# Layer 2's 3x3 convolution re-tiled: three groups of 128 rows, a pair of 58, four image rows at a time

## The chip, the cores and the metric

The kernel runs on one core of a Trainium2 chip. Its time is device time in microseconds for one execution, lower is better. Three executions of the kernel before took 20,867.39, 20,871.12 and 20,881.85 us; the median is 20,871.12 us.

## The reference

Four images of 48 channels and 256 x 256 pixels pass through four residual layers. Before each layer the image is normalised in groups of three channels (the statistics in the kernel). Layers 0, 1 and 3 are gated convolution blocks with 8 x 8 Fourier filters. Layer 2, the one that is changed, is this (cut):

```python
def _L2_conv_ref(x, w1_off, b1_off, w2_off, b2_off, w1_mod, b1_mod, w2_mod, b2_mod):
    integ = jnp.cumsum(jnp.cumsum(x, axis=-1), axis=-2)
    h1 = jax.nn.gelu(_conv(x, w1_off, b1_off, 1), approximate=False)   # 3x3, 48 -> 48
    sub = _conv(h1, w2_off, b2_off, 0)                                  # 1x1, 48 -> 4
    ...                                                                 # a box and its area per pixel
    m1 = jax.nn.gelu(_conv(x, w1_mod, b1_mod, 1), approximate=False)   # 3x3, 48 -> 48
    area = area * _conv(m1, w2_mod, b2_mod, 0)                          # 1x1, 48 -> 48
    A, Bt, Ct, D = four bilinear samples of integ at the box's corners
    return (A + D - Bt - Ct) / area
```

The two 3x3 convolutions share their input, so the kernel computes them as one with 96 outputs; the two 1x1 ones together have 52. All arithmetic is float32.

## The kernel before

Two streams of work are emitted into one program. Stream "a" runs layers 0 and 1 of images 0 to 3 and then layer 3 of all four. Stream "b" runs the first statistics, the weights of layer 1, and layer 2 of each image as soon as its layer 1 is done. `run` advances whichever stream has the smaller clock, a sum of the numbers that each stream yields. Each engine executes its own instructions in program order; the framework orders each engine's list, and some instructions are pinned to the order in which they were written (`pinned`). So layer 2 of an image lies beside layers 0 and 1 of the next one, and layer 2 of the last image beside layer 3. Stream a has five PSUM banks, stream b two (and one for weights).

Layer 2 first builds a table of integral sums in HBM (`sums`). Then it works in 32 pieces of eight image rows per image. For each piece:

- `look` loads, for four rows, the columns of the convolution: which of the 48 channels x 9 taps lie on which partition. `columns` (L290) puts taps of the first two image rows and 16 channels of the third on 112 partitions (tile A, used three times with its columns shifted by dx) and the other 32 channels of the third row with ten rows of masks on 106 partitions (tile B). It issues seven DMAs on ACT's queue (L301 to L305); the tiles have two buffers.
- `convolve` (L941) takes two image rows, 512 pixels: four matmuls of 512 columns (L947) with 112, 112, 112 and 106 rows into one bank, then a Gelu on ACT (L954).
- `project` (L961) multiplies the result with the 1x1 weights (L966) and adds the bias on DVE (L971).
- `boxes` turns the 52 numbers of each pixel into indices and weights; `gather` fetches sums from the table by indirect DMA on GpSimd's queue (L1037), 16 for each of four steps of a piece; `add` weights and adds them on DVE (L1048 to L1051); `finish` transposes the result (L1062) and adds it to the image (L1069).

In the steady loop, step h of piece n gathers for n, adds for the step before, and convolves rows 2h and 2h+1 of piece n+2; it projects the rows of the step before, and the last two rows of a piece at the start of the next piece, just before `boxes`. Odd steps load columns for piece n+3.

Layers 0 and 3 have a convolution of the same kind with another layout: `columns2` (L345) puts 32 channels of the third row on A, 128 partitions, and on B the other 16 channels, twice: 58 partitions for even rows and 58 for odd ones, at partitions 0 and 64. `convolve2` (L420) runs full matmuls (L427) and the tails of 58 rows (L435), two of which stand on different halves of the array. Its loads go to SP's queue (the line of `dma`, L227).

The weights are scaled by the statistics at each layer's start: `normalised_weights` for layer 2, `normalised_weights2` for layers 0 and 3. Both multiply a table of zeros and ones with the statistics (L285, L399) and another table into the mask rows (L335, L413). Layer 2's two tables are loaded once at the start of the program; those of layers 0 and 3 are loaded in each call (L394, L395), into memory that the weights' own preparation (`fused_weights`, ending at L386) used before.

Of the kernel before, what the change touches and what calls it, by code (L numbers as in the profile page):

```python
# [20 lines left out]
CP = 2 * C  # L21
PW = 258
# [36 lines left out]
def constants():  # L59
# [42 lines left out]
    sel = np.zeros((CP, 4, 112))  # L102
    tapsel = np.zeros((112, 4, 106))
    for g in range(4):
        for p in range(112 if g < 3 else 96):
            if g < 3:
                tap, ch = 3 * (p // 48) + g, p % 48
            else:
                tap, ch = 6 + p // 32, 16 + p % 32
            tapsel[p, g, 96 + tap] = 1  # L110
            sel[ch, g, p] = 1


    sel2 = np.zeros((CP, 4, 122))
# [8 lines left out]
    for p in range(48):  # L123
        sel2[32 + p % 16, 3, [10 + p, 74 + p]] = 1
        for q in (0, 64):
            tapsel2[10 + p, 3, q + 6 + p // 16] = 1
    sel2 = np.concatenate([sel2_full.reshape(CP, -1), sel2[:, 3]], 1)
# [35 lines left out]
    for a in range(2):  # L163
# [11 lines left out]
        "c_sel": sel,  # L175
        "c_tapsel": tapsel,
# [12 lines left out]
class Net:  # L189
    def __init__(self, ctx, tc, a, out):  # L190
        self.tc, self.nc, self.a, self.out = tc, tc.nc, a, out
        self.nimage = a["x"].shape[0] // C

        self.banks = {
            f: ctx.enter_context(tc.tile_pool(name="ps" + f, bufs=n, space=PSUM)) for f, n in (("a", 5), ("b", 2))
        }
        self.stream = "a"
        self.const = ctx.enter_context(tc.tile_pool(name="const", bufs=1))
        self.dram = ctx.enter_context(tc.tile_pool(name="dram", bufs=1, space=DRAM))
        self.stat = ctx.enter_context(tc.tile_pool(name="stat", bufs=2))  # L200
        self.n = 0
        nc, a = self.nc, self.a
        self.ident = self.load("c_ident", [128, 128])
        dft = self.load("c_dft", [128, 6, 128])
        self.f1, self.f2, self.a1, self.a2, self.rf, self.ri = (dft[:, i, :] for i in range(6))
        self.sel = self.load("c_sel", [CP, 4, 112])
        self.tapsel = self.load("c_tapsel", [112, 4, 106])
        self.group = self.load("c_group", [CP, CP])
        self.eps = self.const.tile([128, 1], F32, name="eps")
        nc.vector.memset(self.eps[:], 1e-5)  # L210
        self.zero = self.const.tile([CP, PW + 4], F32, name="zero")
        nc.vector.memset(self.zero[:], 0.0)
# [68 lines left out]
    def column_scales(self, mr, pool):  # L281

        ps = self.bank()
        for g in range(4):
            self.nc.tensor.matmul(ps[:112, 2 * g : 2 * g + 2], self.sel[:, g, :], mr[:], start=True, stop=True)  # L285
        t = pool.tile([112, 4, 2], F32, name=self.nm("ms"), tag="ms")
        self.nc.vector.tensor_copy(t[:].rearrange("p a b -> p (a b)"), ps[:112, 0:8])
        return t

    def columns(self, x, r0, n, pool):  # L290

        dma = self.nc.scalar.dma_start
        A = pool.tile([112, n, PW], F32, name=self.nm("A"), tag="A")
        B = pool.tile([106, n, PW], F32, name=self.nm("B"), tag="B")
        row = lambda dy, dx: slice(PW * (r0 + dy) + dx, PW * (r0 + dy + n) + dx)
        flat = lambda t, p0, p1: t[p0:p1].rearrange("p r c -> p (r c)")
        for dy in range(2):  # L300
            dma(flat(A, 48 * dy, 48 * dy + 48), x[0:48, row(dy, 0)])  # L301
        dma(flat(A, 96, 112), x[0:16, row(2, 0)])
        for dx in range(3):
            dma(flat(B, 32 * dx, 32 * dx + 32), x[16:48, row(2, dx)])
        dma(flat(B, 96, 106), self.a["c_inside"][:, PW * r0 : PW * (r0 + n)])  # L305
        return A, B

    def taps(self, AB, pick):

        A, B = AB  # L310
        return [pick(A, dx) for dx in range(3)] + [pick(B, 0)]

    def tap_rows(self):

        got = []
        for dx in range(3):
            got += [(0, 48, dx, dx, 0), (48, 48, dx, 3 + dx, 0), (96, 16, dx, 6 + dx, 0)]
            got.append((32 * dx, 32, 3, 6 + dx, 16))
        return got

    def normalised_weights(self, wb, n, mr, pool):


        nc = self.nc
        t = self.column_scales(mr, pool)
        W = pool.tile([112, 4, n], F32, name=self.nm("W"), tag="W")
        md = pool.tile([112, 4], F32, name=self.nm("md"), tag="md")
        nc.vector.scalar_tensor_tensor(md[:], t[:, :, 0], -1.0, t[:, :, 1], ALU.mult, ALU.mult)
        with self.pool("mt", 1) as sb:
            mt = sb.tile([112, 4, 106], F32, name=self.nm("mt"), tag="mt")  # L330
            ps = self.bank()
            for g in range(4):
                k = 112 if g < 3 else 96
                nc.vector.tensor_scalar(W[:k, g, :], wb[:k, g, :], t[:k, g, 1:2], None, ALU.mult)
                nc.vector.tensor_scalar(mt[:k, g, :], self.tapsel[:k, g, :], md[:k, g : g + 1], None, ALU.mult)  # L335
            for g in range(4):
                k = 112 if g < 3 else 96
                nc.tensor.matmul(ps[:106, :n], mt[:k, g, :], wb[:k, g, :], start=g == 0, stop=g == 3)
        nc.vector.tensor_copy(W[96:106, 3, :], ps[96:106, :n])
        return W  # L340

    def columns2(self, x, r0, n, pool):  # L345
# [4 lines left out]
        for dy in range(3):  # L350
            m = 48 if dy < 2 else 32
            self.dma(flat(A, 48 * dy, 48 * dy + m), x[0:m, row(dy, 0)])
        split = lambda v, q: v.rearrange("p (r q c) -> p r q c", q=2, c=PW)[:, :, q, :]
        for q in range(2):
            self.dma(B[64 * q : 64 * q + 10], split(self.a["c_inside"][:, PW * r0 : PW * (r0 + n)], q))
            for dx in range(3):
                p = 64 * q + 10 + 16 * dx
                self.dma(B[p : p + 16], split(x[32:48, row(2, dx)], q))
# [30 lines left out]
    def normalised_weights2(self, wb, n, mr, pool):  # L389
# [3 lines left out]
        with self.pool("nw", 1) as sb:  # L393
            sel = self.load("c_sel2", [CP, 506], sb)  # L394
            tapsel = self.load("c_tapsel2", [128, 4, 74], sb)  # L395
            ps = self.bank()
            for g in range(4):
                k = 128 if g < 3 else 122
                nc.tensor.matmul(  # L399
                    ps[:k, 2 * g : 2 * g + 2], sel[:, 128 * g : 128 * g + k], mr[:], start=True, stop=True  # L400
# [10 lines left out]
            for g in range(4):  # L411
                nc.vector.tensor_scalar(W[:, g, :], wb[:, g, :], t[:, g, 1:2], None, ALU.mult)
                nc.vector.tensor_scalar(mt[:, g, :], tapsel[:, g, :], md[:, g : g + 1], None, ALU.mult)  # L413
# [498 lines left out]
    def layer2(self, x, mr, y, table):  # L912
# [3 lines left out]
        with ExitStack() as ctx:  # L916
# [3 lines left out]
            wb = w.tile([112, 4, 96], F32, name="wb")  # L920
            for p0, m, g, t, c0 in self.tap_rows():
                self.dma(wb[p0 : p0 + m, g, :], a["L2_w1"][t, c0 : c0 + m, :])
            W = self.normalised_weights(wb, 96, mr, w)
# [10 lines left out]
            kk = [112, 112, 112, 106]  # L934
# [6 lines left out]
            def convolve(t, j):  # L941

                if j == 0:
                    t.sc = sb.tile([128, 16, 52], F32, name="sc", tag="sc", bufs=1)
                ps = self.bank()
                for g, of in enumerate(self.taps(t.G[j // 2], lambda G, d: G[:, 2 * (j % 2) : 2 * (j % 2) + 2, d : d + 256])):
                    m = nc.tensor.matmul(  # L947
                        ps[:96, :].rearrange("p (r c) -> p r c", c=256), W[: kk[g], g, :],
                        of[: kk[g]], start=g == 0, stop=g == 3,
                    )  # L950
                    if g == 0:
                        self.pinned(m)
                t.hm[j] = sb.tile([96, 512], F32, name="hm", tag="hm")
                nc.scalar.activation(t.hm[j][:], ps[:96, :], AF.Gelu, bias=b1[:])  # L954

            def look(t, h):

                if t is not None:
                    t.G[h] = self.columns(x, 128 * t.i + 8 * t.s + 4 * h, 4, cols)

            def project(t, j):  # L961

                ps = self.bank()
                for b in range(4):
# [4 lines left out]
                    if b == 0:  # L969
                        self.pinned(m)  # L970
                self.pinned(nc.vector.tensor_add(  # L971
                    t.sc[:, 4 * j : 4 * j + 4, :], ps[:, 0:208].rearrange("p (k e) -> p k e", e=52),
                    b2[:].unsqueeze(1).to_broadcast([128, 4, 52]),
# [110 lines left out]
            for j in range(4):  # L1084
                convolve(pieces[0], j)
                project(pieces[0], j)
                if j % 2:
                    look(pieces[1], j // 2)
            boxes(pieces[0])
            yield 30  # L1090
            for j in range(4):
                convolve(pieces[1], j)
                if j < 3:
                    project(pieces[1], j)
                if j % 2:
                    look(pieces[2], j // 2)
            yield 30
            last, done = None, None
            for n in range(len(pieces) + 1):
                t = piece(n)  # L1100
                for h in range(4):
# [12 lines left out]
                    if h == 0 and ahead is not None:  # L1114
                        project(ahead, 3)
# [6 lines left out]
                    if t is not None:  # L1122
                        last = (t, h, V)
                        if after is not None:
                            convolve(after, h)
                            if h % 2:
                                look(piece(n + 3), h // 2)
                            if h > 0:
                                project(after, h - 1)
# [242 lines left out]
```

## Time and profile before

| | us |
|---|---|
| median of three executions | 20,871.12 |
| the profiled execution | 20,882.08 |
| its span, first to last instruction | 20,880.3 |
| GpSimd's 8192 indirect DMAs (L1037), busy | 8,227.0 |
| layer 0's and 3's full matmuls (L427), busy | 5,547.3 |
| layer 0's and 3's 58-row tails (L435), busy | 1,271.5 |
| layer 2's convolution: three groups (L947, 112 rows), busy | 1,544.9 |
| layer 2's convolution: fourth group (L947, 106 rows), busy | 527.2 |
| layer 2's projections (L966), busy | 537.0 |
| layer 2's Gelus (L954), busy | 349.4 |

"Busy" is the time in which at least one instruction of the group ran. Matmuls are pipelined and overlap in the records, so a group's busy time is not the time it takes away from others; the step from one instruction's start to the next one's is nearer to that. PE is TensorE's matmuls, PEld its weight loads, DVE VectorE, ACT ScalarE, POOL GpSimd, SP the queue of SyncE; ACTq and SPq are the issuing of DMAs on these engines' queues. "[3.22 <-DVE xt L1069]" behind a line says that the engine stood idle for 3.22 us before it, until line 1069 on DVE had ended. The last layer 2 ends at about 19,840 us; then layer 3 of the last image runs alone.

| DMA queue | packets | MB | share of 16 engines |
|---|---|---|---|
| q1, issued by SP | 1,908,216 | 2084.50 | 38.2% |
| q0, issued by GpSimd | 452,560 | 1110.45 | 21.1% |
| q10, issued by ACT (the columns of layer 2) | 82,944 | 230.48 | 4.4% |

### The profile page before, as it was taken

How to read it: one execution, taken by the hardware profiler on the slowest of the kernel's cores; microseconds unless marked ns; L12 is line 12 of the kernel's file. 1: busy time of each engine (PE TensorE's matmuls, PEld its weight loads, DVE VectorE, ACT ScalarE, POOL GpSimd, SP SyncE). 2: the span in 40 equal slices, each digit the busy share in tenths (PEclk: the TensorE clock that was granted, in tenths of full speed). 3: DMA queues.
4: the chain of work that ended last, by engine and by line, in shares of the span. 5: the costliest groups of instructions: out<-in, count | busy, mean ns of one | idle time of the engine just before them, and what ended most of it. 6: DMA issues, size and time to landing. Idle time of an engine off the chain costs nothing.

```text
span 20880.3 us, 231985 instructions
## 1 busy us (share of the span) xinstructions
PE 18892.3 (90%) x79032; PEld 12001.4 (57%) x79032; DVE 10763.0 (52%) x21931; ACT 5909.3 (28%) x12275; POOL 8637.2 (41%) x8887
## 2 busy tenths in 40 slices
PE   7998798999878989998788899997888999999999
PEld 4565435666533346665433466654334787878888
DVE  4544322477765534677645447776554255555521
ACT  2333312344321123443311234433112211111111
POOL 1000000277754511777555216775552066666600
PEclk9899799999968999999689899996899999999999
DMA  4623886555588975555889755558897566666633
GB/s 114 135 55 82 233 217 194 137 132 134 132 235 230 241 207 139 130 134 127 233 230 240 219 133 130 133 127 229 236 239 225 137 150 151 158 152 160 151 76 74
DMA packets 2444896, 3440.27 MB, mean 165 GB/s; under 512 B 580102, under 2 KB 1997038, under 8 KB 2333179
## 3 DMA queue, kind: packets, MB, share of 16 engines
q1 hardware_dynamic: 1908216, 2084.50, 38.2%
q0 software_dynamic: 452560, 1110.45, 21.1%
q10 hardware_dynamic: 82944, 230.48, 4.4%
q8 instruction: 635, 10.40, 0.2%
q14 instruction: 541, 4.43, 0.1%
HBM read 2486.99 MB, written 802.77 MB: 158 GB/s over the span
## 4 chain that ended last, share of the span: by engine, by line
PE 65%; DMA 15%; DVE 7%; POOL 7%; issue 4%; SPq 1%; ACT 1%; DVEq 0%; ACTq 0%; POOLq 0%
PE ps L427 19%; POOL V L1037 7%; PE ps L947 6%; PE ps L728 5%; PE ps L435 4%; PE ps L741 4%; DMA ct<-cD 4%; PE ps L742 3%; PE ps L697 3%; PE ps L828 3%; DMA hD<-hs 2%; PE ps L1188 2%; DVE V L1050 2%; PE ps L815 1%; PE ps L966 1%
## 5 line engine op out<-in xcount | busy, mean ns | idle before, releaser
L1037 POOL DMA_INDIRECT V<-t,idx x8192 | 8227.0, 1004 | 4897.9 <-issue 2346.8
L427 PE MATMUL ps<-W,A 128*128 128x288 f32 (+1 forms) x24576 | 5547.3, 374 | 85.9 <-DMA A<-x 23.4
L427 PEld LDWEIGHTS ps<-W,A 128*128 128x128 f32 x24576 | 4281.6, 191 | 1226.6 <-issue 523.4
L227 POOL DMA_DIRECT2D X<-x x192 | 144.5, 757 | 4302.6 <-DMA x<-xt 3040.1
L1050 DVE TENSOR_TENSOR V<-V 128x1536 f32<-128x1536 f32 (+3 forms) x2048 | 1839.3, 900 | 19.2
L1048 DVE TENSOR_TENSOR V<-V,w 128x3072 f32<-128x3072 f32 x512 | 1713.3, 3346 | 35.9 <-DMA V<-t,idx 27.0
L728 PE MATMUL ps<-hg,ct 128*128 128x512 f32 x2304 | 1264.4, 676 | 417.5 <-DMA ct<-cD 339.5
L947 PE MATMUL ps<-A,W 112*96 112x512 f32 x3072 | 1544.9, 642 | 26.2 <-DVE xt L1069 21.5
L697 PE MATMUL ps<-win,xp 48*128 48x288 f32 x4096 | 1054.8, 594 | 547.9 <-DVE xp L684 232.4
L508 ACT COPY qkv<-ps 128x288 f32<-128x288 f32 x2048 | 769.9, 400 | 2641.1 <-PE ps L427 1258.4
L435 PE MATMUL ps<-W,B 58*128 58x288 f32 (+1 forms) x8192 | 1271.5, 391 | 26.1 <-DMA B<-x 13.8
L742 PE MATMUL ps<-yh,ht 65*128 65x512 f32 x2304 | 1163.1, 649 | 145.7 <-DMA yh<-ys 111.6
L531 DVE BATCH_NORM_STATS2 bs<-ps 128x6 f32<-128x96 f32 x2048 | 397.4, 251 | 1634.3 <-PE ps L529 1632.3
L741 PE MATMUL ps<-ys,tt 128*128 128x512 f32 x2304 | 1174.1, 632 | 27.6 <-DVE ys L732 25.7
L697 PEld LDWEIGHTS ps<-win,xp 48*128 48x128 f32 x4096 | 647.3, 259 | 924.3 <-ACT hs L704 291.9
L1168 DVE TENSOR_TENSOR gp<-gl,ps 128x192 f32<-128x192 f32 x1024 | 353.8, 351 | 1588.1 <-ACT gl L1167 1579.9
L728 PEld LDWEIGHTS ps<-hg,ct 128*128 128x128 f32 x2304 | 468.0, 211 | 1051.6 <-issue 949.1
L1167 ACT ACTIVATE gl<-ps 128x192 f32<-128x192 f32 x1024 | 332.7, 330 | 2529.4 <-PE ps L427 2245.4
L435 PEld LDWEIGHTS ps<-W,B 58*128 58x128 f32 x8192 | 762.4, 186 | 454.1 <-issue 346.4
L746 DVE TENSOR_TENSOR gt<-gl,ps 128x512 f32<-128x512 f32 x576 | 395.1, 687 | 1142.2 <-PE ps L742 1136.6
L947 PEld LDWEIGHTS ps<-A,W 112*96 112x96 f32 x3072 | 513.9, 176 | 731.4 <-issue 690.3
L742 PEld LDWEIGHTS ps<-yh,ht 65*128 65x128 f32 x2304 | 451.3, 199 | 794.3 <-issue 699.4
(186 smaller groups left out, 24654.4 us busy)
## 6 DMA issues: line engine op xcount, KB each, us to landing
hD<-hs SPq DMA_DIRECT2D x64, 4608.0 KB
hg<-hD SPq DMA_DIRECT2D x288, 1024.0 KB
gD<-gt SPq DMA_DIRECT2D x144, 1024.0 KB
gs<-gD SPq DMA_DIRECT2D x64, 2304.0 KB
V<-t,idx POOLq DMA_INDIRECT x8192
A<-x SPq DMA_DIRECT2D x512, 193.5 KB
xt<-x SPq DMA_DIRECT2D x256, 387.0 KB
A<-x ACTq DMA_DIRECT2D x512, 193.5 KB
```

The lines of the kernel that those rows point to most:

```text
L427: nc.tensor.matmul(to(q, b), A[:, r + q, 128 * b + g : 128 * b + g + 128], W[:, g, :], start=b == 0 and g == 0, stop=b == 1 and g == 2,)
L435: nc.tensor.matmul(to(q, b), B[p, r // 2, 128 * b : 128 * b + 128], W[p, 3, :], start=b == 1, stop=b == 0)
L508: nc.scalar.copy(t.qkv[:, 2 * q + b, :], banks[2 * b + q][:, 0:288])
L697: nc.tensor.matmul(ps[:, :288], xp[64 * h : 64 * h + 48, b, :], win[64 * h : 64 * h + 48], start=True, stop=True,)
L728: nc.tensor.matmul(ps[:].rearrange("p (s n) -> p s n", n=32), ct[:, c, :], hg[:, :, c, :], start=True, stop=True)
L741: nc.tensor.matmul(order(ps[:]), to[:, q, :], pick(yo, 128, q), start=True, stop=False)
L742: nc.tensor.matmul(order(ps[:]), ho[:, q, :], pick(yho, NZ, q), start=False, stop=True)
L828: nc.tensor.matmul(pp[:CP, :], pr[:, q, :], got[q][:], start=q == 0, stop=q == 2)
L947: m = nc.tensor.matmul(ps[:96, :].rearrange("p (r c) -> p r c", c=256), W[: kk[g], g, :], of[: kk[g]], start=g == 0, stop=g == 3,)
L1037: nc.gpsimd.indirect_dma_start(out=V[:, k, 4 * cr : 4 * cr + 4, :].rearrange("p e c -> p (e c)"), out_offset=None, in_=table, in_offset=ba ...
L1048: self.pinned(nc.vector.tensor_mul(Vm, Vm, wm.unsqueeze(2).to_broadcast([128, 64, 48])))
L1050: nc.vector.tensor_add(V[:, :, 0:n, :], V[:, :, 0:n, :], V[:, :, n : 2 * n, :])
```

## The change

Layer 2 now uses `columns2` and `normalised_weights2`, and the older functions go. `columns2` takes the queue on which it issues (ACT's for layer 2): three loads of A and, for each of two halves of B, a mask and three loads, 11 in all. `convolve` takes four image rows: into a first bank rows 0 and 2, into a second rows 1 and 3, each with three full matmuls of 128 rows and one tail of 58; the two tails stand together between the two sets of full ones. Two Gelus follow. `project` still takes one bank's 512 pixels and writes its sums in the order of the rows. In the loop, even steps convolve and load, odd steps project twice; a piece is projected entirely before the step in which `boxes` runs. The two tables are loaded once at the start, for all layers. Layer 2's weights take 15 loads instead of 12 and a memset.

```diff
@@ Net.__init__
-        self.sel = self.load("c_sel", [CP, 4, 112])
-        self.tapsel = self.load("c_tapsel", [112, 4, 106])
+        self.sel = self.load("c_sel2", [CP, 506])
+        self.tapsel = self.load("c_tapsel2", [128, 4, 74])
...
-    def columns2(self, x, r0, n, pool):
+    def columns2(self, x, r0, n, pool, dma=None):
+        dma = dma or self.dma
         A = pool.tile([128, n, PW], F32, name=self.nm("A"), tag="A")
         B = pool.tile([122, n // 2, PW], F32, name=self.nm("B"), tag="B")
...
@@ normalised_weights2
-            sel = self.load("c_sel2", [CP, 506], sb)
-            tapsel = self.load("c_tapsel2", [128, 4, 74], sb)
...
@@ layer2
-            wb = w.tile([112, 4, 96], F32, name="wb")
-            for p0, m, g, t, c0 in self.tap_rows():
+            wb = w.tile([128, 4, 96], F32, name="wb")
+            nc.vector.memset(wb[:, 3, :], 0.0)
+            for p0, m, g, t, c0 in self.tap_rows2():
                 self.dma(wb[p0 : p0 + m, g, :], a["L2_w1"][t, c0 : c0 + m, :])
-            W = self.normalised_weights(wb, 96, mr, w)
+            W = self.normalised_weights2(wb, 96, mr, w)
...
-            def convolve(t, j):
+            def convolve(t, h):
 
-                if j == 0:
+                if h == 0:
                     t.sc = sb.tile([128, 16, 52], F32, name="sc", tag="sc", bufs=1)
-                ps = self.bank()
-                for g, of in enumerate(self.taps(t.G[j // 2], lambda G, d: G[:, 2 * (j % 2) : 2 * (j % 2) + 2, d : d + 256])):
-                    m = nc.tensor.matmul(
-                        ps[:96, :].rearrange("p (r c) -> p r c", c=256), W[: kk[g], g, :],
-                        of[: kk[g]], start=g == 0, stop=g == 3,
-                    )
-                    if g == 0:
-                        self.pinned(m)
-                t.hm[j] = sb.tile([96, 512], F32, name="hm", tag="hm")
-                nc.scalar.activation(t.hm[j][:], ps[:96, :], AF.Gelu, bias=b1[:])
+                A, B = t.G[h]
+                ps = [self.bank() for _ in range(2)]
+                to = [p[:96, :].rearrange("p (r c) -> p r c", c=256) for p in ps]
+                for q in range(2):
+                    for g in range(3):
+                        m = nc.tensor.matmul(
+                            to[q], W[:, g, :], A[:, q:4:2, g : g + 256],
+                            start=q == 0 and g == 0, stop=q == 1 and g == 2,
+                        )
+                        if q == 0 and g == 0:
+                            self.pinned(m)
+                    if q == 0:
+                        for i in range(2):
+                            p = slice(64 * i, 64 * i + 58)
+                            nc.tensor.matmul(to[i], W[p, 3, :], B[p, :, 0:256], start=i == 1, stop=i == 0)
+                for q in range(2):
+                    t.hm[2 * h + q] = sb.tile([96, 512], F32, name="hm", tag="hm")
+                    nc.scalar.activation(t.hm[2 * h + q][:], ps[q][:96, :], AF.Gelu, bias=b1[:])
...
-                    t.G[h] = self.columns(x, 128 * t.i + 8 * t.s + 4 * h, 4, cols)
+                    t.G[h] = self.columns2(x, 128 * t.i + 8 * t.s + 4 * h, 4, cols, nc.scalar.dma_start)
...
@@ the loop of layer2
                     if h == 0 and ahead is not None:
-                        project(ahead, 3)
                         boxes(ahead)
...
                         if after is not None:
-                            convolve(after, h)
-                            if h % 2:
+                            if h % 2 == 0:
+                                convolve(after, h // 2)
                                 look(piece(n + 3), h // 2)
-                            if h > 0:
-                                project(after, h - 1)
+                            else:
+                                for j in range(2):
+                                    project(after, h - 1 + j)
                     yield 11
```

## The prediction

> **What bounds the kernel now.** I read the page's busy shares and its chain of waits first, then busy times by stretch, then TensorE's instructions one by one.
>
> ```profile
> PE 18892.3 (90%) x79032; PEld 12001.4 (57%) x79032; DVE 10763.0 (52%) x21931; ACT 5909.3 (28%) x12275; POOL 8637.2 (41%) x8887
> PE 65%; DMA 15%; DVE 7%; POOL 7%; issue 4%; SPq 1%; ACT 1%; DVEq 0%; ACTq 0%; POOLq 0%
> ```
>
> TensorE is busy 90% and carries 65% of the chain; the convolution to be changed (L947) is 5.8% of it. Layer 2 always runs beside something else, and what limits differs by stretch (span, PE, PEld, DVE, ACT, POOL, clock, DMA share, GB/s):
>
> ```profile
> 4000.00:5700.00 1700.00, 1625.56 (x6414) 1012.19 (x6414) 1184.44 (x2653) 673.78 (x1410) 1170.48 (x1149) 0.98 0.52 130
> 5700.00:6330.00 630.00, 464.48 (x1477) 247.96 (x1474) 397.15 (x683) 180.46 (x293) 344.36 (x357) 0.66 0.81 231
> 6330.00:7430.00 1100.00, 962.78 (x2229) 409.99 (x2227) 573.50 (x836) 184.68 (x304) 581.56 (x614) 0.90 0.91 237
> 16560.00:19700.00 3140.00, 3032.23 (x18721) 2498.80 (x18720) 1683.69 (x3016) 586.20 (x1319) 1983.37 (x2027) 0.98 0.66 154
> ```
>
> Beside layer 0 (first row) and layer 3 (last row) PE is busy 96%; beside layer 1's two parts (rows two and three) it is 74% and 88%, and DMA is nearly full. Rows one to three recur for two more images. The same view for L947's instructions alone counts 608, 168, 248 and 1024 of them in the four stretches (282, 108, 116 and 471 us of PE).
>
> Every float32 matmul is two records (two passes). L947 has 4096, and 16 make four image rows: 256 tiles of four rows, of which 3×38=114 lie beside layer 0, 3×10.5=31.5 and 3×15.5=46.5 beside layer 1, 64 beside layer 3.
>
> **The convolution.** Durations overlap, so the price is the step from one weight load to the next. The first two rows are L947 at full clock, the next two a pair of 58-row matmuls of layer 0, the last two one such matmul alone:
>
> ```profile
> 4526.58 0.16 PEld L947 LDWEIGHTS ps<-A,W 112*96 112x96 f32 x1 [0.27 <-issue]
> ...
> 4528.72 0.16 PEld L947 LDWEIGHTS ps<-B,W 106*96 106x96 f32 x1 [0.27 <-issue]
> ...
> 4026.61 0.30 PEld L435 LDWEIGHTS ps<-W,B 58*128 58x128 f32 x4 [0.79 <-issue]
> 4027.30 1.02 PEld L427 LDWEIGHTS ps<-W,A 128*128 128x128 f32 x5 [0.39 <-issue]
> ...
> 4470.03 0.29 PEld L435 LDWEIGHTS ps<-W,B 58*128 58x128 f32 x2 [0.39 <-issue]
> 4470.70 0.78 PEld L427 LDWEIGHTS ps<-W,A 128*128 128x128 f32 x4 [0.39 <-issue]
> ```
>
> 4526.58 to 4528.72 is five steps: 0.428 us for 512 columns. Layer 0's full matmuls of 288 columns step 0.243 us. The pair's four passes take 4027.30−4026.61=0.69 us: two steps of 0.243 plus 0.20, so the halves of the array run together; the lone one's two passes take 0.67, the same. The 0.20 is the price of going to half-array matmuls and back.
>
> Four rows cost 16×0.428=6.85 us now, and 12×0.428+(2×0.428+0.20)=6.20 after: 0.66 less. The compiled order of the changed kernel has 239 pairs side by side and 17 apart; those cost 2×1.06 instead of 4×0.428, 0.40 more. 239×0.66−17×0.40=151 us of PE, 0.59 per tile.
>
> A rule speaks against this: the Trainium skill, TensorEngine Tiling (Array Packing), Key Properties, says a change of tiling mode drains TensorE, with no figure; its Theoretical Speedup gives up to 2×. At 2× the sum would be 256×0.86=219 us; the rows with their 0.20 give 166 before the split pairs. I take the rows, because they contain the drain.
>
> What of it shortens the span:
> - Beside layer 0: 114×0.59=67 us. GpSimd is close behind (1170 us busy and 322 between gathers, of 1700; the chain in this stretch is 27% gathers), so I count 65%: 44.
> - Beside layer 3: 64×0.59=38; PE lines carry over 85% of its chain: 34.
> - Layer 1's first part: 31.5×0.59 at clock 0.66 instead of 0.98 is 28; PE idles 26% behind copies and stores, so half: 14.
> - Its second part: 46.5×0.59=27; loads of ct and yh hold PE, so 0.3: 8.
>
> Together 100.
>
> **Tables once.** Sixteen loads leave SP's queue. They matter where layer 3 begins:
>
> ```profile
> 17520.90 0.31 SPq L227 DMA_DIRECT2D c_sel_sb<-c_sel  x1
> 17521.26 0.42 SPq L227 DMA_DIRECT2D c_tapsel_sb<-c_tapsel  x1
> ...
> 17525.21 1.82 PE L399 MATMUL ps<-mr,c_sel_sb 96*128 96x2 f32 x8 [23.16 <-DMA c_tapsel_sb<-c_tapsel]
> ```
>
> The loads issue when L386 has ended (17,520.87), since they reuse its memory. L399 then waits 4.3 us for them and runs 1.8; both go. The other 17 us of the 23 is the weights' own loads and stays. PE waits so at three layer starts (54.2 us in all): 3×6=18. At the other starts no such wait shows: nothing; if one becomes the last wait, under 5 us each.
>
> **Loads of columns, on ACT's queue.** A look becomes 11 issues instead of 7:
>
> ```profile
> 4513.90 0.31 ACTq L301 DMA_DIRECT2D A<-x  x1
> 4514.25 0.43 ACTq L302 DMA_DIRECT2D A<-x  x1
> 4514.78 1.32 ACTq L304 DMA_DIRECT2D B<-x  x3
> 4516.14 0.37 ACTq L305 DMA_DIRECT2D B<-c_inside  x1
> ```
>
> Now 2×0.31+0.43+1.32+0.37=2.74 us; after, with six B at 0.44, two masks at 0.37 and three A, 4.4: +1.7 us × 256. Against it, Gelus come in twos and compiled table loads fall from 336 to 246: 90×1.28=115 us of ACT saved. Behind an issue stand layer 0's qkv and qs copies or layer 3's gl, and PE needs the banks they free. Four of the 11 stand ahead of the second Gelu, while PE still convolves; behind it 7 to 9 remain, where 6 are now: 0.4 to 1.3 us later. ACT is busy 40% of the first stretch, and PE waits there only 2.4 us for its largest item, qs. Ends: nothing, or 1.7×178=300 us if every issue beside layers 0 and 3 reaches PE. The waits are near nothing, so I take 25.
>
> Bytes fall: 218 rows of 4128 B become 128 of these and 232 of 1032, 900 to 768 KB. The Trainium skill, DMA: Bandwidth & Descriptors, Bandwidth, calls transfers under 64 KB descriptor-dominated and gives 0.68 us for 4 KB, 0.95 for 64 KB. An estimate from it: eight small ones of about 0.8 us replace three of about 1.1 and a mask, +2 us a look, and 46.5 looks fall where DMA is full: +100. The queue table says otherwise: ACT's queue moves 230.48 MB in 4.4% of the engines' time, SP's, with packets of 1.1 KB instead of 2.8, 2084.50 MB in 38.2%: 52 and 55 MB per percent. By that a look saves 132 KB, 0.56 us at 237 GB/s: 26 us there, half of it counted 10 with what PE saves already taken. I take the row; ends −26 and +100.
>
> **The rest.** A convolution takes both PSUM banks of its stream, then two projections follow one another. PE stands still for L1069's additions 21.5+31.2 us in all; where two transposes come just before two projections, the convolution no longer lies between them and 3.4 us of cover go, at 64 strips: from −20 (projections precede boxes by half a step) to +100; near the present waits, +15. GpSimd issues 12 more weight loads of 0.5 us, once per image three: +5. The projection's addition writes in another order with the same 208 values: nothing.
>
> **Sum:** −100−18−10+25+15+5=−83. The profiled execution took 20,882.1 us (span 20,880.3), 11 above the median of 20,871: 20,799 becomes **20,790**.
>
> **Rivals.**
> - *Gathers pace layer 0's stretches* (15%): nothing there, and the waits cost 60 instead of 45: −56−18−10+60=−24, 20,850. For it, GpSimd's 27% of the chain; against, PE's 96%.
> - *All of it counts* (15%): 67+38+28+20+18+10=181, waits near 10: 20,700.
> - *ACT's issues stop PE* (9%, slower): in each of 178 looks the copy behind the last issue is late, stream a's five banks run out, and PE stands for the 1.7 us: −128+303+20=+195, 21,065. It decides from 0.7 us per look. Against: ACT's slack.
> - *The pairs run in turn* (4%, the change not doing what it says): 0.20 more for 256 tiles, +51, and −28+45: 20,940. Against: the 0.69.
>
> My forecast has 57%. Faster: 0.57+0.15=0.72; within 0.2%, about what a measurement can tell: 0.15; slower: 0.13. The range 20,690 to 20,900 takes in the first two rivals and the smaller waits and leaves out the two slow ones.
>
> **What would show it.** The tails' four passes taking 1.06 us; PE about 150 us less busy; no wait of L399's successor on a table; PE's waits on qs, qkv and gl still small. A sum of such waits above 130 us, or a stretch beside layer 0 still 1700 long with PE less busy, would prove me wrong.

## The result, and the profile after

The changed kernel took 20,767.55 us (median of five runs, 20,746.18 to 20,843.95), the kernel before, run beside it, 20,871.12 (20,852.44 to 20,887.15): a ratio of 0.9953, 95% interval 0.9941 to 0.9965, or 104 us less. The forecast was 20,790. Its sum is nearly right and most of its terms are not, as the experiments show.

The page of the changed kernel, the lines that answer to the first two shown of before:

```profile
PE 18830.0 (91%) x79032; PEld 11956.8 (58%) x79032; DVE 10830.0 (52%) x21947; ACT 5784.0 (28%) x12185; POOL 8656.1 (42%) x8899
PE 72%; DMA 14%; DVE 6%; POOL 4%; issue 2%; SPq 1%; ACT 1%; ACTq 0%; DVEq 0%; POOLq 0%
```

TensorE is busy 62 us less, not 150. The stretches are compared from event to event, not at fixed times. First the kernel before, for its second image: layer 1's first, second and third part, then layer 0 of the third image, then all of layer 3 (columns as before: span, then PE, PEld, DVE, ACT, POOL, clock, DMA share, GB/s):

```profile
5699.30:6268.70 569.40, 410.46 (x1361) 225.35 (x1361) 365.21 (x626) 170.21 (x276) 317.19 (x328) 0.63 0.81 232
6268.70:7440.70 1172.00, 1017.58 (x2345) 433.27 (x2346) 609.65 (x898) 194.94 (x321) 609.43 (x643) 0.90 0.91 236
7440.70:7791.50 350.80, 299.25 (x1393) 186.73 (x1394) 126.01 (x270) 111.86 (x219) 14.12 (x20) 0.92 0.71 209
7791.50:9901.40 2109.90, 2026.43 (x8267) 1292.86 (x8266) 1344.03 (x3068) 825.54 (x1793) 1202.74 (x1189) 0.98 0.52 131
16198.00:20872.00 4674.00, 4491.49 (x28190) 3790.02 (x28190) 2051.34 (x3782) 893.73 (x2056) 2106.52 (x2159) 0.98 0.58 134
```

Then the changed one, the same five stretches:

```profile
5689.10:6240.70 551.60, 408.72 (x1360) 238.40 (x1360) 375.48 (x626) 173.19 (x277) 335.88 (x345) 0.62 0.86 243
6240.70:7418.80 1178.10, 1017.86 (x2336) 430.23 (x2336) 608.40 (x898) 193.90 (x320) 606.89 (x634) 0.89 0.91 232
7418.80:7747.50 328.70, 292.61 (x1386) 182.37 (x1387) 124.74 (x266) 111.47 (x218) 12.68 (x18) 0.95 0.72 216
7747.50:9848.00 2100.50, 2010.95 (x8280) 1276.76 (x8278) 1355.27 (x3076) 784.17 (x1764) 1189.18 (x1186) 0.98 0.52 129
16089.00:20758.00 4669.00, 4492.11 (x28229) 3783.80 (x28227) 2063.74 (x3791) 892.26 (x2060) 2112.51 (x2164) 0.97 0.59 133
```

Over all images the stretches changed so: layer 1's first part -47 us, its second +25, its third -68, layer 0 -20, layer 3 -6; with 2 us at the start these are the 115 between the two traces' ends. The third part, where no layer 2 runs, gave most. It ends with the next layer's weights, and there the loads of the tables stood. Layer 3, where the forecast put 52 us, gave almost nothing.

### The profile page after: what moved, and what is told of

It is laid out like the page before. It is cut to its first block, busy times and chain, and to the rows that moved or that the text cites. A ratio compares the mean times of both kernels' runs of the same rounds, so it can differ in the third digit from the quotient of the medians.

```text
span 20765.8 us, 232624 instructions
## 1 busy us (share of the span) xinstructions
PE 18830.0 (91%) x79032; PEld 11956.8 (58%) x79032; DVE 10830.0 (52%) x21947; ACT 5784.0 (28%) x12185; POOL 8656.1 (42%) x8899
## 4 chain that ended last, share of the span: by engine, by line
PE 72%; DMA 14%; DVE 6%; POOL 4%; issue 2%; SPq 1%; ACT 1%; ACTq 0%; DVEq 0%; POOLq 0%
PE ps L353 22%; PE ps L361 5%; PE ps L876 5%; PE ps L654 4%; POOL V L974 3%; PE ps L668 3%; PE ps L667 3%; DMA ct<-cD 3%; PE ps L623 3%; PE ps L754 3%; PE ps L1120 2%; PE ps L901 2%; PE ps L811 2%; PE ps L505 2%; DMA A<-x 2%
## 5 line engine op out<-in xcount | busy, mean ns | idle before, releaser
L876 PE MATMUL ps<-A,W 128*96 128x512 f32 x3072 | 1483.5, 619 | 3.0 <-issue 3.0
L876 PEld LDWEIGHTS ps<-A,W 128*96 128x96 f32 x3072 | 487.2, 168 | 853.4 <-issue 839.6
L658 DVE COPY ys<-ps 128x512 f32<-128x512 f32 x576 | 397.2, 690 | 1086.0 <-PE ps L654 897.3
```

Source lines behind the costliest of these rows:

```text
L876: m = nc.tensor.matmul(to[q], W[:, g, :], A[:, q:4:2, g : g + 256], start=q == 0 and g == 0, stop=q == 1 and g == 2,)
```

## The experiments

All ran beside the kernel before on the same chip. Four chips were met: one for experiments 1 to 4 and one for 5 to 8, both with a granted clock of about 0.92 (before: 20,884.8 and 20,857.2 us), and one each for 9 and 10 and for 11 and 12, which granted 0.84 (25,694 and 25,632 us). On these last two more than the clock differs: TensorE's waits sum to about 5,200 us, against 1,900 in the changed kernel's first trace, and for 2,100 of them the profile names nothing that was waited for. So what a whole kernel shows there need not hold on the other chips. Across chips ratios are compared; where differences of medians are given too, this is said.

**1. Tables once, on the kernel before.**

```diff
@@ Net.__init__
-        self.tapsel = self.load("c_tapsel", [112, 4, 106])
+        self.tapsel = self.load("c_tapsel", [112, 4, 10])
+        self.sel2 = self.load("c_sel2", [CP, 506])
+        self.tapsel2 = self.load("c_tapsel2", [128, 4, 74])
...
@@ normalised_weights2
-            sel = self.load("c_sel2", [CP, 506], sb)
-            tapsel = self.load("c_tapsel2", [128, 4, 74], sb)
+            sel, tapsel = self.sel2, self.tapsel2
```

> The kernel before, layer 2 unchanged, with the two tables for paired columns loaded once (the old tapsel kept as its ten non-zero columns, so that all four tables fit). The prediction's theory: only the waits at three layer-3 starts go, -18 us, about 20,853. Its rival, from the two traces: the loads also held up VectorE where layer 0 follows layer 1 (L386's product stands on VectorE's queue ahead of stream b's sums), and the four stretches after layer 1 lost 68 us and the turns between layer 3's images 16: -70 to -85 us, 20,785 to 20,800. A third: the 68 us belong to the new loop or the layout, and this gives -13 to -20.

20,634.8 us, ratio 0.9890 (0.9874 to 0.9906): 250 us faster than the kernel before beside it, beyond every expectation. By stretch, the third parts and the starts in them gave -62 us, and layer 1's second part, which the edit does not touch, went from 902.3, 1172.0, 1179.2 and 1162.7 to 841.6, 1127.8, 1126.4 and 1122.9. The first of the four has no layer 2 beside it. This called for an explanation of its own (5 to 9).

**2. The changed kernel with those two loads back in each call of layers 0 and 3.**

```diff
         with self.pool("nw", 1) as sb:
+            sel, tapsel = self.sel, self.tapsel
+            if n != 96:
+                sel = self.load("c_sel2", [CP, 506], sb)
+                tapsel = self.load("c_tapsel2", [128, 4, 74], sb)
             ps = self.bank()
```

> The changed kernel with the tables of layers 0 and 3 loaded in each call again. The prediction's theory: +18 us on the changed kernel's 20,768, about 20,786. The rival: +70 to +85, 20,838 to 20,853, with layer-0 starts again 17 us longer each. If the first experiment shows much and this one little, the new loop had a part in it.

20,857.6 us, ratio 0.9988 (0.9979 to 0.9997), against 0.9953 for the changed kernel: +73 us by the ratios, +90 by the medians of two chips. The prediction's 18 falls.

**3. The two tails apart.**

```diff
-                    if q == 0:
-                        for i in range(2):
-                            p = slice(64 * i, 64 * i + 58)
-                            nc.tensor.matmul(to[i], W[p, 3, :], B[p, :, 0:256], start=i == 1, stop=i == 0)
+                        if g == 2 - 2 * q:
+                            p = slice(64 * q, 64 * q + 58)
+                            nc.tensor.matmul(to[q], W[p, 3, :], B[p, :, 0:256], start=False, stop=q == 0)
```

> The changed kernel with the two tails of a tile never side by side: the first behind the third full matmul of the first bank, the second behind the first full matmul of the second bank. The prediction's theory: two tails apart take 2x1.06 us instead of 1.06, 239 x 1.06 = 253 us of TensorE, and by its shares of the span (65%, 90%, half, 0.3) +167 us: 20,935. The rival, that TensorE's time near layer 2 counts half as much as the shares say (layer 3's stretches and layer 1's second part gained nothing from the pairs): +80, 20,850.

20,996.0 us, ratio 1.0059 (1.0045 to 1.0074): +221 us by the ratios, +228 by the medians. The pair does run side by side. A tile whose instructions stand together takes 7.55 us (median, from its first matmul to the next instruction) instead of 6.36: the 1.19 more are two steps of 0.428 and a second switch of 0.33. In all TensorE's steps of the convolution, waits left out, rose by 293 us. Three quarters of that became span, where the prediction's shares came to 167 of 253, two thirds. The rival, that TensorE's time near layer 2 counts half as much, falls. Then the layout's gain should be seen too, unless something gives it back.

**4. The new loop and tables once, with the old columns** (`columns`, `taps` and `normalised_weights` of before).

```diff
+                for q in range(2):
+                    for g, of in enumerate(self.taps(t.G[h], lambda G, d: G[:, 2 * q : 2 * q + 2, d : d + 256])):
+                        m = nc.tensor.matmul(to[q], W[: kk[g], g, :], of[: kk[g]], start=g == 0, stop=g == 3)
```

> The changed kernel's loop (two banks, two Gelus, look, two projections) and tables loaded once, with the old columns of 112, 112, 112 and 106 rows: 16 records of 512 columns per four rows, seven loads per look. The prediction's theory: the layout was worth 100 us of convolution and 10 of bytes and cost 25 for issues, so 85 more than the changed kernel: 20,853. The rival, by the stretches of the two traces without the starts (layer 1's first part -46, second +20, layer 0 -20, layer 3 +7): 30 to 45 more, about 20,805, with layer 1's second part back at 1,163 to 1,172 us per image and its first part at 569 if these come from the layout; if the loop made them, they stay at 1,178 and 554.

20,589.1 us, ratio 0.9862 (0.9846 to 0.9878): faster than the changed kernel by 190 us by the ratios, 178 by the medians. Taken alone it would say that the new layout costs 180. But its second parts are the short ones again: 838.5, 1138.0, 1122.2 and 1133.9.

**What 1 and 4 share** is the place of the data. Their tables take 5160 bytes per partition, those of before and after 3488 and 3208, and stream a's tiles lie behind these constants. Four kernels move them by 32 bytes:

```diff
         nc.vector.memset(self.eps[:], 1e-5)
+        pad = self.const.tile([128, 1], F32, name="pad")
+        nc.vector.memset(pad[:], 0.0)
```

**5. On the changed kernel.**

> The changed kernel with one unused constant of 4 bytes per partition (it takes 32) ahead of all of stream a's working tiles, so that these move by 32 bytes: layer 1's second part then has ht, hg, ct, tt and gt at multiples of 64 bytes, as the first and fourth experiment have, where the kernels before and after have them 32 bytes off. Theory (place in memory): layer 1's second part falls from 907.6, 1178, 1180 and 1176 us to about 840, 1130, 1125 and 1125, packets of 512 B from 30.6 to 27.6 ns: -200, about 20,570. Rival (the compiled order or the old layout made the 45 us per image): nothing changes, 20,768.

20,775.9 us, ratio 0.9964 (0.9951 to 0.9978): nothing. Multiples of 64 bytes are not the point.

**6. On the kernel before.**

> The kernel before with the same unused constant of 32 bytes, nothing else. Theory (place in memory): -190, about 20,685, though no instruction of layers 0 to 3 is another. Rival: 20,875, as before.

20,862.0 us, ratio 1.0000 (0.9991 to 1.0009): nothing.

**7. On the first experiment.**

> The first experiment (tables once on the kernel before) with the same constant, which puts layer 1's tiles back 32 bytes off, as in the kernel before. Theory (place in memory): the second part takes 1172 us again, and what is left is the tables' own worth: 20,634 + 190 = 20,825, -50 to -80 against before (the prediction's -18 would be 20,853). Rival: 20,635.

20,809.9 us, ratio 0.9979 (0.9970 to 0.9989). By the ratios, thirty-two unused bytes took back 186 us of the first experiment's 230 (by the medians of two chips 175 of 250); the second parts are 891.9, 1163.4, 1158.3 and 1161.0 again. What stays is the tables' worth: -47 us on this chip, between 23 and 63 by the interval.

**8. On the fourth.**

> The fourth experiment (new loop, old columns, tables once) with the same constant, so 32 bytes off, as the changed kernel is. Now only the layout differs from the changed kernel. Theory (place in memory): 20,589 + 200 = 20,790, so the layout is worth 20 us or so; by the prediction's 100 - 25 + 10 it would be 85 above the changed kernel, 20,853. Rival (the new layout itself costs 180): 20,589.

20,781.8 us, ratio 0.9969 (0.9957 to 0.9981): 223 us lost by the ratios, 193 by the medians. Now 6, 7, 8 and 5 form a ladder on one chip, all without the good placement: before 1.0000, tables once 0.9979, with the new loop 0.9969, with the new layout 0.9964. The new loop is worth some 28 us by the medians, the new layout 6, each less than its interval. As far as these runs can tell, the convolution, the core of the change, brought next to nothing.

**9. The changed kernel with layer 1's second part moved alone** to the addresses that it has in 1 and 4:

```diff
             w = ctx.enter_context(self.pool("wb", 1))
             sb = ctx.enter_context(self.pool("bb", 2))
+            pad = w.tile([128, 488], F32, name=self.nm("pad"))
+            nc.vector.memset(pad[:, 0:1], 0.0)
```

> The changed kernel with 1952 unused bytes per partition at the head of the pool of layer 1's second part, and nothing else moved: that part's tiles then lie at the very addresses that they have in the first and fourth experiment (hts at 69,888, hg at 76,032, ct at 92,416, tt at 96,512, gt at 102,656). Theory (place in memory, of this part's tiles alone): second parts of about 840, 1130, 1125 and 1130 us instead of 907.6, 1178, 1180 and 1176, and packets of 512 B of 27.6 ns, so -200: 20,570. Rival (the order of work or the first layers' tiles made the 45 us): 20,770.

25,611.1 us, ratio 0.9964 (0.9950 to 0.9979), on a chip with a granted clock of 0.836. The first image's second part ran before that chip's clock fell. It took 854.3 us, against 910.3 for experiment 10 beside it. The view of DMA in 2400 to 3150 us, inside that part, has first the ninth kernel and then the tenth (packets, MB, share of 16 engines):

```profile
q1 hardware_dynamic: 147036, 173.15, 84.7%
```

```profile
q1 hardware_dynamic: 137097, 161.13, 79.3%
```

Seven per cent more passed in the same time. In the trace's records of single packets in this window, those of 512 B (gt's stores, tt's and ht's loads) take 27.5 to 27.6 ns on average in 1, 4, 9, 11 and 12, nearly all of them 27; in the others (before, after, 2, 3, 5 to 8, 10) 30.5 to 31.3, about a tenth of them at 41. So the place is the cause of the shorter part: one pool was moved, and but for the pad's memset no instruction of layer 1 is another. With the short packets hts, hg, ct, tt and gt start at multiples of 256 bytes; with the long ones 96 (before, after, 2, 3, 10), 128 (5, 6) or 32 bytes (7, 8) beyond one. The Trainium skill, DMA: Bandwidth & Descriptors, How a descriptor splits into AXI transactions, says that a transaction has to start at a 256-byte boundary and that longer descriptors are split into transactions of 256 B. An estimate from it: 512 B off a boundary need three instead of two. These runs agree in which places are fast. But about four in five packets off the boundary still took 25 to 29 ns, which no run here explains. No second multiple of 256 was tried, so that this is the property is likely and not shown.

The whole kernel did not gain the 200 us that were expected. After the first image, where this chip's clock fell, the other three second parts took 1434, 1389 and 1442 us, against 1448, 1431 and 1444 in experiment 10: 57 us together.

**10. Four more loads on ScalarE's queue in each look.**

```diff
+                    more = cols.tile([16, 4, 2, 129], F32, name=self.nm("more"), tag="more", bufs=1)
+                    r = 8 * t.s + 4 * h
+                    for k in range(4):
+                        nc.scalar.dma_start(more[:, k], ...)   # two rows of 129 values on 16 partitions
```

> The changed kernel with four more loads on ScalarE's queue in each look (16 rows of 516 B pairs, of no use to the result), so 15 issues of it instead of 11: the step from 7 to 11 done once more, with less data. The prediction's theory: +25 us for four issues, 20,795, its ends 0 and 300. Rival: the paired layout gains 94 us of convolution steps against the old one (fourth and eighth experiment) and 12 in all, so that issues and small packets give back 80: +60 to +100, 20,830 to 20,870, most of it in layer 1's second part and in layer 0.

25,816.3 us, ratio 1.0048 (1.0032 to 1.0064), 205 us above experiment 9 beside it. But that one has the faster placement; in the stretches where it should not matter (layer 1's first part, layer 3, and layer 0 beside layer 2) the difference of the two traces is 69 us, 61 of it beside layer 0. TensorE's waits for ScalarE rose by 38 there, and by 11 in all. It leans to the rival, on a chip on which the changed kernel itself was not run.

**11. Experiment 9 once more.**

> The ninth experiment's kernel once more, since the chip of that run granted a clock of 0.83 over the whole program and its 854.3 us for the first image's second part (910.3 in its neighbour) told the place's worth only there. Theory (place in memory): at a granted clock of 0.92 all four second parts fall as in the first and fourth experiment, and the kernel takes 20,570. Rival: 20,770 but for some 50 us of the first image, 20,720.

25,562.4 us, ratio 0.9978 (0.9965 to 0.9991): again a chip that granted 0.837, and again a short second part for the first image, 849.3 us. So the expected 20,570, which was for a clock of 0.92, was not put to the test. What the placement is worth to the changed kernel as a whole at a clock of 0.92 stays open; the two pairs that show it there for other kernels, 1 with 7 and 4 with 8, say 186 and 223 by the ratios.

**12. The small loads put together, beside 11.**

```diff
@@ columns2, for layer 2 (cut)
+                v = x[32:48, two(2, 0)]
+                v = type(v)(v.tensor, v.offset, [[1, 3]] + [list(d) for d in v.ap])
+                dma(flat(B, 64 * q + 10, 64 * q + 58), v)
...
@@ convolve
-                            to[q], W[:, g, :], A[:, q:4:2, g : g + 256],
+                            to[q], W[:, g, :], A[:, 2 * q : 2 * q + 2, g : g + 256],
```

`two(2, 0)` takes rows 2q and 2q + 1 of the four, and the added dimension of `v` the three shifts.

> The kernel of the run beside it, with each look's small loads put together: the first bank takes image rows 0 and 1 of the four and the second 2 and 3 (not 0, 2 and 1, 3), so that a tail's two rows are contiguous, its three shifts are one load of 48 packets of 2064 B, and its mask one load of 10. A look is 7 issues and 244 packets again, not 11 and 360; TensorE's instructions are the same. The prediction's theory: four issues fewer give back its 25 us, 20,545 if the run beside it takes 20,570. Rival (issues and small packets gave back 80 of the layout's gain): -60 to -100 against the run beside it, in layer 1's second part and in layer 0.

25,382.8 us, ratio 0.9900 (0.9882 to 0.9918): 180 us below experiment 11, the intervals apart. Seven issues instead of eleven, with matmuls of the same shapes on other rows, are worth more than either theory said, on this chip. The way it comes about is not shown. A look takes 5.9 us from its first issue to its last, not 8.8, but TensorE's waits for ScalarE fell by 26 us only (866 to 840), and all its waits together are the same (5,193 and 5,196). In the traces its instructions outside the convolution took 164 us less; the granted clock was 0.838 to 0.840 in these runs and 0.835 to 0.838 in those of experiment 11.

## Why the prediction came out right, and where it was wrong

The forecast was right in sign, and near in size by luck, because errors cancelled: the convolution was to bring 85 net and brought about 6; the tables were to bring 18 and brought 47 to 73; the new loop was to cost 15 in waits and brought about 28, if anything. On the chip of experiments 5 to 8 the three came to 81 us, where the forecast had 83.

**The tile's steps: the drain was too small.** The prediction took the pair for two steps and 0.20 us. This is the timeline of weight loads of the changed kernel, for one whole tile beside layer 0:

```profile
4060.22 0.16 PEld L876 LDWEIGHTS ps<-A,W 128*96 128x96 f32 x1 [0.27 <-issue]
...
4062.37 0.16 PEld L876 LDWEIGHTS ps<-A,W 128*96 128x96 f32 x1 [0.27 <-issue]
4063.31 0.25 PEld L885 LDWEIGHTS ps<-B,W 58*96 58x96 f32 x4 [0.79 <-issue]
4064.35 0.24 PEld L876 LDWEIGHTS ps<-A,W 128*96 128x96 f32 x2 [0.79 <-issue]
...
4066.58 0.19 PEld L901 LDWEIGHTS ps<-w,hm 96*128 96x128 f32 x1 [0.27 <-issue]
```

L885's four passes step on after 1.04 us, as foretold (1.06). But the whole tile, 4060.22 to 4066.58, takes 6.36, which is also the median beside layers 0 and 3. Twelve steps of 0.428 leave 1.22 for the tails: two steps and 0.36. The drain is paid on both sides of the pair, and 0.69 us from the first tail's load to the next full one had shown one side. So 0.49 per tile instead of 0.66. The drain for which the Trainium skill, TensorEngine Tiling (Array Packing), Key Properties, has no figure comes to 0.36 us for a pair here.

**What of it shortens the span: beside layer 0 the gain went to ScalarE, elsewhere to several takers.** Experiment 8 has the same loop with the old columns. These are its rows for the second image's second part, for layer 0 and for layer 3:

```profile
6234.90:7402.90 1168.00, 1021.80 (x2337) 438.38 (x2338) 608.47 (x899) 194.28 (x320) 604.42 (x635) 0.90 0.89 236
7731.70:9828.70 2097.00, 2022.96 (x8279) 1293.12 (x8277) 1353.03 (x3072) 786.84 (x1764) 1187.78 (x1184) 0.98 0.51 132
16058.00:20739.00 4681.00, 4515.16 (x28221) 3806.87 (x28220) 2062.45 (x3787) 894.05 (x2060) 2113.47 (x2161) 0.98 0.58 134
```

The following sums are from the traces' records of single instructions. From one matmul's start to the next, waits left out, the convolution's steps sum to 122 us less in the changed kernel (beside layer 0 52, layer 3 30, layer 1's parts 15 and 26), and to 111 less in experiment 5, which ran on experiment 8's chip. Yet the two traces are 19 and 28 us longer than that of experiment 8. TensorE's waits took 92 us back (78 in experiment 5). Its other instructions, which are the same but for layer 2's weights, took 52 (66), at a lower granted clock. Some 30 of these can be the chance of the profiled execution: experiment 8's was 33 us below its median, at 0.922, the highest clock of its runs. But over the runs too the clock is lower, 0.918 to 0.919 in experiment 5 against 0.919 to 0.922 in experiment 8. Whether the layout lowers it was not tested.

Of the waits, those for ScalarE rose from 181 to 282 us (277 in experiment 5): +101, where the prediction put 25 on the kernel before (197). Beside layer 0 they rose by 46 and took nearly all of the 52; those for VectorE fell by 36 in all. The loop with old columns first, then the changed kernel (us, times, longest):

```profile
PE ps L706 <- ACT hs L713: 109.1, 110, 8.8
PE ps L436 <- ACT qs L525: 5.5, 3, 1.9
PE ps L521 <- ACT qkv L517: 2.3, 3, 1.0
PE ps L750 <- ACT ys L743: 1.5, 2, 0.8
```

```profile
PE ps L623 <- ACT hs L630: 142.5, 99, 9.3
PE ps L667 <- ACT ys L660: 25.1, 13, 6.9
PE ps L438 <- ACT qkv L434: 21.9, 12, 4.6
PE ps L353 <- ACT qs L442: 18.2, 11, 3.9
```

These are the copies that stand behind a look on ScalarE. Their sum beside layers 0 and 3 stayed under the 130 us that were to disprove me, since I had not counted layer 1's hs and ys. The issues themselves were sized well: 2.88 us per look in experiment 8, 4.66 after, +1.8 against 1.7. What was missed is that the queue also stops between issues. From the first to the last a look took 5.6 us, now 9.0. ScalarE's timeline of the changed kernel shows a long one:

```profile
4492.45 0.44 ACTq L283 DMA_DIRECT2D B<-c_inside  x1
4492.93 2.73 ACTq L286 DMA_DIRECT2D B<-x  x3
4499.22 0.30 ACTq L283 DMA_DIRECT2D B<-c_inside  x1
4499.56 3.02 ACTq L286 DMA_DIRECT2D B<-x  x3
4502.62 0.70 ACT L434 COPY qkv<-ps 128x288 f32<-128x288 f32 x2 [9.97 <-DMA B<-x]
```

The B loads take 0.9 to 1.0 us each here, 3.6 us pass between the third and the next mask, and the qkv copies stand for 9.97 us. The rival "ACT's issues stop PE" thus had the mechanism, at about 0.4 us per look instead of 1.7 (a quarter of a microsecond beside layers 0 and 3, of which it spoke); its point of decision was 0.7. Beside layer 0 the other test came half true: the three stretches are 20 us shorter (44 forecast) with TensorE busy 53 us less, so its idle time grew.

**Tables once: another wait stood in front of theirs.** I counted TensorE's waits on the table's DMA and found them at layer 3 only. At layer 0's starts no such wait showed, and I priced them at nothing. DVE, SP's queue and TensorE of before (three views of one start):

```profile
3568.13 1.35 DVE L386 TENSOR_TENSOR wh<-wh,wd 128x1152 f32<-128x1152 f32 x1
...
3585.19 0.17 DVE L404 COPY ms<-ps 128x6 f32<-128x6 f32 x1 [3.49 <-PE ps L399]
```

```profile
3569.51 0.31 SPq L227 DMA_DIRECT2D c_sel_sb<-c_sel  x1
```

```profile
3580.43 3.78 PE L885 MATMUL ps<-c_down_sb,X 128*128 128x129 f32 x16 [7.53 <-DVE X L878]
3584.00 1.15 PE L399 MATMUL ps<-mr,c_sel_sb 96*128 96x2 f32 x8
3585.01 1.58 PE L885 MATMUL ps<-c_down_sb,X 128*128 128x129 f32 x12
3586.43 2.10 PE L415 MATMUL ps<-wh,mt 128*74 128x288 f32 x8
...
3598.52 2.13 PE L427 MATMUL ps<-W,A 128*128 128x288 f32 x4
```

The tables' loads are issued when L386 ends, at 3569.5, and L399 starts 14.5 us later. No wait on them shows because L885 of stream b, ahead of L399 on TensorE, waits for VectorE's X until 3580.4 (such waits sum to 102 us). With the tables loaded once (experiment 7) L403, its L399, ran at the start:

```profile
3533.19 1.83 PE L403 MATMUL ps<-mr,c_sel_sb 96*128 96x2 f32 x8
...
3561.72 2.10 PE L419 MATMUL ps<-wh,mt 128*74 128x288 f32 x8
...
3574.69 3.08 PE L431 MATMUL ps<-W,A 128*128 128x288 f32 x12
```

From L386's end the first full matmul came after 29.0 us before and after 15.9 here. The four third parts, which contain these starts, are 70 us shorter in that trace. At layer 3's turns, where the prediction looked, three came out 1.1, 3.4 and 8.5 us shorter (from one image's last full matmul to the next one's first): 13 of its 18, and 23 in experiment 7.

**Bytes and small packets.** I counted -10 by the queue table's row; the rule of transfer sizes gave +100. Layer 1's second part, where DMA is full, is 25 us longer than before and 22 longer than in experiment 8. Against the latter, TensorE's waits for DMA rose by 27 us there and those for ScalarE (ys) by 23; in experiment 5 by 47 and 13. The sign is the rule's, the size nearer to the row.

**The waits for L1069's additions** were to add 15. L901 waits 45.1 us on them, against 52.7: nothing added, and the loop as a whole gained some 28 instead of losing. **GpSimd's weight loads** (+5) are not visible.

**Layer 3** gained 6, not 52. Its convolution steps, waits left out, fell by 35 us, and its waits, the turns among them, by 6. But TensorE's other instructions took 35 us more (52 in experiment 5), at a granted clock of 0.972 instead of 0.975 over these stretches. The last image, with no layer 2 beside it, took 970.8 instead of 955.9 us; but experiment 6, which is the kernel before moved by 32 bytes, took 965.3 for it, so some 9 us of these 15 are scatter between executions.

## What to carry to other kernels

A total that agrees proves none of its terms: undo the parts one at a time, and compare a matmul saved with what its loads add to the queue that issues them, measured from the first issue to the last. A load that nobody seems to wait for can still be last, if another wait on the same engine covers it. Before an edit that moves constants is given credit, run the same kernel shifted by some bytes. And read the granted clock beside every difference of a few tenths of a per cent.

## What was not expected of the hardware

Thirty-two bytes of unused constant cost 186 and 223 us of 20,600 by the ratios (1 and 7, 4 and 8) and changed no instruction of the layers. A switch to half-array matmuls and back cost 0.36 us.

The granted clock went with the kernel and not only with the chip. On the chips of experiments 1 to 8 the kernel before had 0.921 to 0.923 in every run, those with the paired columns (2, 3 and 5) 0.914 to 0.921; on the other two chips it was 0.840 to 0.844 against 0.832 to 0.840. Why is not shown.

The fastest kernel measured at a clock of 0.92 is the fourth, 20,589 us (ratio 0.9862, 0.9846 to 0.9878): the new loop and the tables without the new columns, in the good place. The twelfth, which has the new columns, the good place and merged loads, was run only on a chip granting 0.84, where it takes 0.9900 of the kernel before; the two were not run side by side.
